# A Mamba and mixture-of-experts kernel: the first guess of each root on one engine, and the block plan's numbers on VectorE

## The chip, the core and the metric

The kernel runs on one core of a Trainium2 chip. A core has a matrix engine (TensorE, PE in the profile; PEld is its weight loads), VectorE (DVE), ScalarE (ACT), GpSimd (POOL) and SyncE (SP), which here only issues transfers. Each engine works through a queue of its own in order; engines wait for each other by semaphores. The metric is the device time of one execution in microseconds. Before the change three runs gave 1625.85, 1628.82 and 1631.47 us, median 1628.82.

## The reference

Input x is 4 sequences of 1024 tokens, 256 wide, all in float32. Two layers follow each other, each with its residual and a layer norm behind it.

```python
h = x * rsqrt(mean(x*x) + 1e-5) * norm_scale
xs, res = split(h @ w_in, 2)                      # 512 channels each
xs = silu(causal_conv(xs, conv_w, 4 taps) + conv_b);  res = silu(res)
delta, B, C = split(xs @ w_xproj, [16, 32])
delta = softplus(delta @ w_dt + b_dt)
s[t] = exp(delta[t] * A) * s[t-1] + delta[t] * xs[t] * B[t]   # 512 channels x 16 states
y = sum over the 16 states of s * C
x = layernorm(2 * x + ((y + xs * D) * res) @ w_out)

n = x * rsqrt(mean(x*x) + 1e-8) * norm_weight
p = sigmoid(n @ router.T);  the best 2 of 8 experts, weights p / (sum of both + 1e-6)
x = layernorm(x + shared_mlp(n) + sum over both of weight * expert_mlp(n))
```

Each MLP is 256 to 1024 to 256 with a relu and biases.

## The kernel before

**Chunks and stages.** A sequence is cut into two chunks of 512 tokens, eight chunks in all. For a chunk, `front` computes the first norm, the projections, the convolution and delta; then 16 scan steps, one for each state n, run over the four blocks of 128 channels (`inputs`, `scan`, `outputs`); then `tail` computes the gate, the output projection, both norms and the routing, and `by_expert` scatters the tokens to the rows of their experts and plans blocks of 128 rows. `moe` works through units of 128 rows, four of the shared MLP and some routed blocks for each chunk. `finish` is the closing layer norm over all tokens, in five pieces.

**A scan step.** PE spreads a row of B or C over the partitions (L427). DVE multiplies three of the four channel blocks by B (L441), POOL the fourth (L446). ACT computes da = exp(delta * A) (L454), DVE runs the recurrence (L457, four a step) and multiplies by C (L470), POOL adds that to y (L471, 128x2048 elements). The product hs has three buffers, da has two in PSUM.

**What runs beside it.** While chunk i is scanned, `front` of chunk i+1, `tail` of chunk i-1 and the units of `moe` are issued in between as generators: after each channel block, the main loop advances them. Which instruction of an engine is issued before which is then settled when the program is built: the framework takes the program order as priority and lets an instruction go when its inputs are there by its own estimate of durations, so that an instruction can go ahead of one written before it, or behind one written after it. Some ACT and DVE instructions are pinned by `keep_in_program_order`.

**The roots.** `rsqrt(v, name, engine)` is called 21 times: in `front` for the mean square `ms` that ACT computed (eight, 128x4 numbers, on POOL but for the first chunk, which uses DVE), in `tail` for both variances of the norms (eight, 128x8, on POOL, from a `var` that POOL computes in L520 to L522), and in `finish` (five, the last on DVE, the others on POOL). It treats the float as an integer: a shift right by one (L204) and a subtraction from a constant (L206) give the first guess, both on DVE, whatever `engine` is. Three Newton steps of four instructions follow on `engine` (L209 to L212).

**The plan.** `by_expert` has the counts of tokens by expert in `place`, a part of one PSUM tile (`pr`). DVE compares them with the multiples of 128 (L681) and sums to the number of full blocks so far (L686); POOL subtracts the blocks done (L687) and multiplies by a triangular matrix of ones, 8x8 for each partition (L689). Then the first choice's four scatters are issued (POOL's indirect DMAs, L646), and after a pause of a turn or two the second choice's. DVE sums the products to each expert's first block (L696) and goes on to the table `plan` (L697 to L721), from which SP's queue reads the expert of a block (L767) and the place of its rows (L793). POOL adds to `done` (L726). Eight plans are made, the last behind the last scan.

The main loop's share that issues `moe`:

```python
            side(ending)
            other_work(LEN[b, c] / MAXC)
```

Of the kernel before, what the change touches and what calls it, by code (L numbers as in the profile page):

```python
# [10 lines left out]
ALU = mybir.AluOpType  # L11
AX = mybir.AxisListType

P = 128
# [6 lines left out]
E = 8  # L21
# [44 lines left out]
I32, U32 = mybir.dt.int32, mybir.dt.uint32  # L66
# [4 lines left out]
def mamba_moe_kernel(  # L71
# [18 lines left out]
    nc = tc.nc  # L90

    const = ctx.enter_context(tc.tile_pool(name="const", bufs=1))
    small = ctx.enter_context(tc.tile_pool(name="small", bufs=2))
# [49 lines left out]
    before = const.tile([P, E, E], F32, tag="before", name="before")  # L143
# [56 lines left out]
    def rsqrt(v, name, engine=nc.gpsimd):  # L200

        shape = list(v.shape)
        half = small.tile(shape, I32, tag="half", name=f"half_{name}")
        nc.vector.tensor_scalar(half, v.bitcast(I32), 1, None, ALU.logical_shift_right)  # L204
        y = small.tile(shape, F32, tag="root", name=f"root_{name}")
        nc.vector.tensor_scalar(y.bitcast(I32), half, -1.0, float(0x5F3759DF), ALU.mult, ALU.add)  # L206
        t = small.tile(shape, F32, tag="nt", name=f"nt_{name}")
        for _ in range(3):
            engine.tensor_tensor(t, y, y, ALU.mult)  # L209
            engine.tensor_tensor(t, t, v, ALU.mult)  # L210
            engine.tensor_scalar(t, t, -0.5, 1.5, ALU.mult, ALU.add)  # L211
            engine.tensor_tensor(y, y, t, ALU.mult)  # L212
        return y
# [47 lines left out]
    def front(b, c):  # L261
# [9 lines left out]
        for t in range(TT):  # L271
            nc.scalar.activation(
                hn[:, t, :], x_sb[:, t, :], AF.Square, accum_out=ms[:, t : t + 1]
            )
        nc.scalar.activation(ms, ms, AF.Identity, bias=eps, scale=1.0 / D)
        rstd = rsqrt(ms, f"r1_{s}", nc.vector if alone else nc.gpsimd)
        for _ in range(3):
            yield
# [203 lines left out]
    def tail(b, c):  # L482
# [38 lines left out]
        nc.gpsimd.tensor_scalar(var[:, 1, :], var[:, 0, :], 1e-8, 0.0, ALU.mult, ALU.add)  # L521
        nc.gpsimd.tensor_tensor(var[:, 1, :], var[:, 1, :], mv[:, :, 1], ALU.add)  # L522
        rstd = rsqrt(var, f"l1_{s}")
        yield from wait(3, 6)
        hn = one.tile([P, TT, W], F32, tag="hn2", name=f"hn2_{s}")
# [87 lines left out]
        nc.scalar.copy(combT, pc)  # L613
        channels[b, c] = (x1T, combT)
        yield from by_expert(b, c, hn, rank, weights, both, sofar, part, flat)

    def by_expert(b, c, hn, rank, weights, both, sofar, part, flat):
# [6 lines left out]
        place = part(TT + 1, E)  # L624
# [18 lines left out]
        def scatter(i):  # L643
            nc.gpsimd.tensor_copy(hn[:, :, WEIGHT : WEIGHT + 1], weights[:, i, :].unsqueeze(2))
            for t in range(TT):
                ins = nc.gpsimd.indirect_dma_start(  # L646
                    rows_of[:, :],
                    bass.IndirectOffsetOnAxis(to[:, i, t : t + 1].bitcast(U32), 0),
                    hn[:, t, :], None,
                ).ins  # L650
                for other in scatters:
                    tc.declare_no_dep(ins, other, reason="no two choices share a row")
                for other in taken_from:
                    tc.declare_no_dep(ins, other, reason="rows behind those of full blocks")
                scatters.append(ins)
# [21 lines left out]
        done = done_of[0]  # L677
        levels = [P, E, CAP // BS]
        over = one.tile(levels, F32, tag="ahead", name=f"over_{s}")
# [3 lines left out]
            level.unsqueeze(1).to_broadcast(levels), ALU.is_gt if last_chunk else ALU.is_ge,  # L683
        )
        there = one.tile([P, E], F32, tag="there", name=f"there_{s}")
        nc.vector.tensor_reduce(there, over, AX.X, ALU.add)  # L686
        nc.gpsimd.tensor_tensor(there, there, done, ALU.subtract)  # L687
        ee = one.tile([P, E, E], F32, tag="ee", name=f"ee_{s}")
        nc.gpsimd.tensor_tensor(ee, before, there.unsqueeze(1).to_broadcast([P, E, E]), ALU.mult)  # L689
        scatter(0)  # L690
        yield from wait(1, 2)
        scatter(1)
# [34 lines left out]
        else:  # L727
            over = one.tile([P, 1], I32, tag="over", name="blocks_over")
# [11 lines left out]
    half = HB // 2  # L740
# [201 lines left out]
    def finish():  # L942
# [34 lines left out]
        for i, (o, dst) in enumerate(pieces):  # L977
            tiles = o.shape[1]
            mv = small.tile([P, tiles, 2], F32, tag="mv2", name=f"mv2_{i}")
            stats(o, mv, slice(0, tiles), f"l2_{i}")  # L980
            var = small.tile([P, tiles], F32, tag="var2", name=f"var2_{i}")
            nc.vector.tensor_scalar(var, mv[:, :, 1], 1e-5, None, ALU.add)
            newton = nc.gpsimd if i + 1 < len(pieces) else nc.vector
            rstd = rsqrt(var, f"l2_{i}", newton)
            shift = small.tile([P, tiles], F32, tag="shift", name=f"shift_l2_{i}")
            newton.tensor_tensor(shift, mv[:, :, 0], rstd, ALU.mult)
            newton.tensor_scalar(shift, shift, -1.0, 0.0, ALU.mult, ALU.add)
            if ahead is not None:
                scale(*ahead)
            ahead = o, dst, rstd, shift  # L990
# [34 lines left out]
    for i, step in enumerate(order):  # L1025
        b, c, n = step
        place = chunks.index((b, c))
# [40 lines left out]
    left = nc.values_load(blocks_over[0][0:1, 0:1], min_val=0, max_val=len(at_end))  # L1068
# [66 lines left out]
```

## Time and profile before

| | |
|---|---|
| median of three runs | 1628.82 us (1625.85 to 1631.47) |
| the profiled execution | 1626.85 us |
| its span, first to last instruction | 1625.2 us |
| mean granted clock of PE | 0.87 |
| busy: PE, DVE, ACT, POOL | 1216.2, 1306.5, 1069.7, 1160.6 us |
| last scan ends | 1396 us |
| DMA | 211.59 MB, 130 GB/s on average |

The costliest groups of the page, as line, engine, operation, tiles, shapes and count, then busy time and the mean in ns of one, then the engine's idle time just before them and what ended most of it:

```profile
L471 POOL TENSOR_TENSOR y<-y,hs 128x2048 f32<-128x2048 f32 x128 | 593.8, 4639 | 79.5 <-DVE hs L470 75.2
L457 DVE TENSOR_TENSOR_SCAN hs<-da,state,hs 128x512 f32<-128x512 f32 x256 | 318.0, 1272 | 17.9 <-ACT da L454 17.3
L470 DVE TENSOR_TENSOR hs<-hs,pb 128x2048 f32<-128x2048 f32 x128 | 291.1, 2275 | 4.2 <-PE pb L427 3.0
```

Busy time counts an instruction from its start to its end, so one that is held after it has started looks long rather than late. Idle time is counted before an instruction and put down to the one whose semaphore came last.

### The profile page before, as it was taken

What the parts mean: (1) busy time and instruction counts of PE and PEld (TensorE: products, weight loads), DVE (VectorE), ACT (ScalarE), POOL (GpSimd) and SP (SyncE); (2) the same over time, 40 slices, a digit from 0 to 9 for tenths busy, and PEclk for the clock granted to TensorE, in tenths of its full rate; (3) what the DMA queues carried; (4) which work ended last, traced back from release to release, by engine and by line L of the source; (5) the groups of instructions that cost most, each with busy time, mean ns of one, the idle gap of its engine ahead of it and who ended that gap; (6) DMA issues with size and microseconds to landing.
All of it is one profiled execution on the core that took longest, in us unless ns stands there. A gap on an engine that the chain in (4) does not pass through costs nothing. (4 is left out here: it accounts for less than half of the span.)

```text
span 1625.2 us, 19982 instructions
## 1 busy us (share of the span) xinstructions
PE 1216.2 (75%) x6216; PEld 918.9 (57%) x6216; DVE 1306.5 (80%) x1451; ACT 1069.7 (66%) x2353; POOL 1160.6 (71%) x896
## 2 busy tenths in 40 slices
PE   5253147875668788978878987788888888899990
PEld 2011023663246666666656755676667677789990
DVE  3899899889997898889998998899999889520005
ACT  5656647785678667777688667876786676354442
POOL 1478986698668876798779976997699787641123
PEclk8585576987789899889999998899899899999995
DMA  4000000151015562366326630574166437559996
GB/s 144 0 0 0 0 13 14 59 172 38 20 35 181 173 185 75 117 202 185 81 66 201 209 105 35 165 240 121 34 192 187 136 90 249 180 167 308 335 278 215
DMA packets 160272, 211.59 MB, mean 130 GB/s; under 512 B 20617, under 2 KB 138130, under 8 KB 160162
## 3 DMA queue, kind: packets, MB, share of 16 engines
q1 hardware_dynamic: 135954, 181.75, 33.6%
q0 software_dynamic: 17216, 21.57, 7.4%
q10 hardware_dynamic: 6992, 6.95, 1.2%
q8 instruction: 51, 0.84, 0.2%
q14 instruction: 59, 0.48, 0.1%
HBM read 178.97 MB, written 31.27 MB: 129 GB/s over the span
## 5 line engine op out<-in xcount | busy, mean ns | idle before, releaser
L471 POOL TENSOR_TENSOR y<-y,hs 128x2048 f32<-128x2048 f32 x128 | 593.8, 4639 | 79.5 <-DVE hs L470 75.2
L454 ACT ACTIVATE da<-delta,chan_sb 128x512 f32<-128x512 f32 x512 | 353.4, 694 | 205.7 <-DVE hs L457 202.2
L868 PE MATMUL pd<-w,h 128*128 128x256 f32 x1600 | 387.8, 387 | 18.0 <-ACT h L848 11.3
L868 PEld LDWEIGHTS pd<-w,h 128*128 128x128 f32 x1600 | 300.0, 194 | 91.6 <-issue 23.6
L457 DVE TENSOR_TENSOR_SCAN hs<-da,state,hs 128x512 f32<-128x512 f32 x256 | 318.0, 1272 | 17.9 <-ACT da L454 17.3
L457 DVE TENSOR_TENSOR_SCAN hs<-da,hs 128x512 f32<-128x512 f32 x256 | 302.7, 1212 | 27.9 <-ACT da L454 27.5
L839 PEld LDWEIGHTS pu<-xT,w 128*128 128x128 f32 x2176 | 270.8, 200 | 64.4 <-ACT xT L822 45.4
L839 PE MATMUL pu<-xT,w 128*128 128x128 f32 x2176 | 276.5, 284 | 26.6 <-ACT xT L822 26.6
L470 DVE TENSOR_TENSOR hs<-hs,pb 128x2048 f32<-128x2048 f32 x128 | 291.1, 2275 | 4.2 <-PE pb L427 3.0
L848 ACT ACTIVATE h<-pu,wb 128x128 f32<-128x128 f32 x800 | 228.8, 368 | 74.1 <-PE pu L839 66.5
L446 POOL TENSOR_TENSOR hs<-xs,b 128x512 f32<-128x512 f32 x144 | 199.8, 1392 | 86.9 <-ACT b L439 64.8
L441 DVE TENSOR_TENSOR hs<-xs,pb 128x1536 f32<-128x1536 f32 (+1 forms) x128 | 213.9, 1671 | 15.3 <-ACT b L439 8.8
L427 PE MATMUL pb<-parts,pick 128*128 128x512 bf16 x256 | 107.0, 421 | 150.7 <-DVE hs L441 60.0
L901 POOL DMA_INDIRECT sums<-rb,xb x68 | 108.2, 1591 | 133.8 <-ACT h L848 41.4
L293 PE MATMUL pi<-hT,w_in_sb 128*128 128x512 f32 x256 | 150.4, 719 | 41.8 <-DVE xs L325 15.1
L839 PEld LDWEIGHTS pu<-x1T,w 128*128 128x128 f32 x1024 | 138.5, 213 | 19.4 <-issue 10.9
L839 PE MATMUL pu<-x1T,w 128*128 128x128 f32 x1024 | 143.5, 299 | 0.0
L219 DVE BATCH_NORM_STATS2 bnst_l<-o 128x6 f32<-128x256 f32 x32 | 12.1, 413 | 145.7 <-DMA o<-sums 145.7
L293 PEld LDWEIGHTS pi<-hT,w_in_sb 128*128 128x128 f32 x256 | 52.5, 221 | 127.5 <-issue 39.9
L439 ACT COPY b<-pb 128x512 f32<-128x512 f32 x128 | 75.5, 590 | 30.1 <-PE pb L427 27.0
L503 PE MATMUL po<-w_out_sb,y 128*128 128x256 f32 x256 | 70.3, 437 | 31.8 <-POOL y L493 27.0
L427 PEld LDWEIGHTS <-pick 128*128 128x128 bf16 x256 | 26.6, 107 | 111.1 <-DVE hs L441 51.7
(187 smaller groups left out, 1401.4 us busy)
## 6 DMA issues: line engine op xcount, KB each, us to landing
w<-in_ew SPq DMA_DIRECT2D x136, 1024.0 KB
w<-in_sw SPq DMA_DIRECT2D x16, 1024.0 KB
xb<-rows SPq DMA_DIRECT2D x68, 129.0 KB
x<-in_x SPq DMA_DIRECT2D x8, 512.0 KB
sums<-summed ACTq DMA_DIRECT2D x8, 512.0 KB
sums<-rs POOLq DMA_DIRECT2D x16, 256.0 KB
o<-sums SPq DMA_DIRECT2D x3, 1024.0 KB
out<-o ACTq DMA_DIRECT2D x3, 640.0 KB
```

Source lines behind the costliest of these rows:

```text
L293: nc.tensor.matmul(pi, lhsT=w_in_sb[:, k, m * P : (m + 1) * P], rhs=hT[:, k, :], start=(k == 0), stop=(k == KD - 1),)
L427: nc.tensor.matmul(pb, lhsT=pick[:, row : row + 1].to_broadcast([P, P]), rhs=scans[b, c][3], start=True, stop=True,)
L441: nc.vector.tensor_tensor(hs[:, 0:on_pool, :], xs[:, 0:on_pool, :], pb.unsqueeze(1).to_broadcast([P, on_pool, TC]), ALU.mult,)
L446: nc.gpsimd.tensor_tensor(hs[:, k, :], xs[:, k, :], copy, ALU.mult)
L454: nc.scalar.activation(da, delta[:, k, :], AF.Exp, scale=chan_sb[:, k, CA + n : CA + n + 1])
L457: nc.vector.tensor_tensor_scan(hs[:, k, :], da, hs[:, k, :], 0.0 if c == 0 else state[:, k, n : n + 1], ALU.mult, ALU.add,)
L470: nc.vector.tensor_tensor(hs, hs, pb.unsqueeze(1).to_broadcast([P, KB, LEN[b, c]]), ALU.mult)
L471: nc.gpsimd.tensor_tensor(y, y, hs, ALU.add)
L839: nc.tensor.matmul(pu[:, i, :], lhsT=w[:, k, at : at + P], rhs=xT[:, k, :], start=(k == 0), stop=(k == KD - 1),)
L848: nc.scalar.activation(t[:, i, :], pu[:, i, :], AF.Relu, bias=wb[:, m : m + 1])
L868: nc.tensor.matmul(pd, lhsT=hidden[h][:, i, :], rhs=w[:, m, :], start=(m == 0), stop=(m == HB - 1 and e is None),)
L901: nc.gpsimd.indirect_dma_start(sums_of[:, :], bass.IndirectOffsetOnAxis(xb[:, TOKEN : TOKEN + 1].bitcast(U32), 0), rb, None, compute_op=AL ...
```

## The change

`rsqrt` makes its first guess in one instruction on `engine`: the integer times -0.5 plus the constant, instead of a shift and a product with -1 plus the constant on DVE. The tile `half` is gone. In `by_expert` the number of full blocks is summed into PSUM (`so_far`, over the first row of `place`, which has been read by then); DVE subtracts the blocks done twice, once into `there` (SBUF, read later by L697 and L725) and once into `left` (PSUM, the second row of `place`), and multiplies `left` by the triangular matrix. POOL no longer takes part ahead of the scatters.

```diff
     def rsqrt(v, name, engine=nc.gpsimd):
 
         shape = list(v.shape)
-        half = small.tile(shape, I32, tag="half", name=f"half_{name}")
-        nc.vector.tensor_scalar(half, v.bitcast(I32), 1, None, ALU.logical_shift_right)
         y = small.tile(shape, F32, tag="root", name=f"root_{name}")
-        nc.vector.tensor_scalar(y.bitcast(I32), half, -1.0, float(0x5F3759DF), ALU.mult, ALU.add)
+        engine.tensor_scalar(
+            y.bitcast(I32), v.bitcast(I32), -0.5, float(0x5F3759DF), ALU.mult, ALU.add
+        )
         t = small.tile(shape, F32, tag="nt", name=f"nt_{name}")
...
         there = one.tile([P, E], F32, tag="there", name=f"there_{s}")
-        nc.vector.tensor_reduce(there, over, AX.X, ALU.add)
-        nc.gpsimd.tensor_tensor(there, there, done, ALU.subtract)
+        so_far, left = place[:, 0, :], place[:, 1, :]
+        nc.vector.tensor_reduce(so_far, over, AX.X, ALU.add)
+        nc.vector.tensor_tensor(there, so_far, done, ALU.subtract)
+        nc.vector.tensor_tensor(left, so_far, done, ALU.subtract)
         ee = one.tile([P, E, E], F32, tag="ee", name=f"ee_{s}")
-        nc.gpsimd.tensor_tensor(ee, before, there.unsqueeze(1).to_broadcast([P, E, E]), ALU.mult)
+        nc.vector.tensor_tensor(ee, before, left.unsqueeze(1).to_broadcast([P, E, E]), ALU.mult)
         scatter(0)
```

## The prediction

> **What bounds the kernel now.** I read the page first, then the windows, then who waits for whom, then the lines that the change touches. The busy line of the page says that VectorE (DVE) is the fullest engine, but it is an average over stages, so the first cut is by stage; the columns are the window, then busy time (and instructions) of PE, PEld, DVE, ACT, POOL, the granted clock, DMA share and GB/s:
>
> ```profile
> PE 1216.2 (75%) x6216; PEld 918.9 (57%) x6216; DVE 1306.5 (80%) x1451; ACT 1069.7 (66%) x2353; POOL 1160.6 (71%) x896
> ...
> 0.00:40.00 40.00, 23.71 (x40) 9.07 (x40) 14.88 (x42) 22.32 (x56) 8.11 (x48) 0.84 0.48 146
> 40.00:1396.00 1356.00, 1008.48 (x4970) 741.12 (x4970) 1252.84 (x1254) 956.73 (x2021) 1086.65 (x733) 0.86 0.36 110
> 1396.00:1420.00 24.00, 19.20 (x100) 16.79 (x100) 8.81 (x18) 4.72 (x18) 10.07 (x12) 0.86 0.42 128
> 1420.00:1585.00 165.00, 162.61 (x1102) 150.29 (x1101) 8.32 (x35) 74.57 (x241) 42.13 (x48) 1.00 0.87 271
> 1585.00:1626.00 41.00, 2.25 (x11) 1.64 (x9) 21.64 (x104) 11.32 (x22) 13.62 (x58) 0.57 0.65 213
> ```
>
> From 40 to 1396 us, until the last scan, DVE is busy 1252.8 of 1356 us; PE, ACT and POOL have 348, 399 and 269 us free there. From 1420 to 1585 us PE works off the expert blocks that are left, 162.6 of 165 us busy. The last 41 us are the closing norm. The order of PE's work follows the scans up to 1396 us, so what DVE saves there moves the later stages forward. The waits say the same; each line is who waited, for whom, the total, the times and the longest (first all engines, then DVE alone from 40 to 1396 us):
>
> ```profile
> ACT da L454 <- DVE hs L457: 202.2, 212, 4.4
> ```
>
> ```profile
> DVE hs L457 <- ACT da L454: 44.8, 20, 5.6
> DVE pr L696 <- POOL ee L689: 12.2, 4, 4.3
> DVE hs L441 <- POOL y L471: 4.8, 2, 2.4
> DVE half_l L204 <- POOL var L522: 1.2, 2, 0.6
> ```
>
> ACT waits for the scans 202 us, the scans for ACT 45 us. The second and fourth line are waits that the change touches. The instructions of the first guess, by source line (shortest, median and longest duration in ns):
>
> ```profile
> L204 DVE TENSOR_SCALAR half_l<-var x13: 154/171/743, 238.8 to 1614.1; 128x8 int32<-128x8 int32 x11, 128x4 int32<-128x4 int32 x2
> L204 DVE TENSOR_SCALAR half_r<-ms x8: 157/492/3555, 6.9 to 941.2; 128x4 int32<-128x4 int32 x8
> ...
> L206 DVE TENSOR_SCALAR root_l<-half_l x13: 140/171/3362, 241.1 to 1614.4; 128x8 int32<-128x8 int32 x11, 128x4 int32<-128x4 int32 x2
> ```
>
> An instruction over four to eight numbers takes 0.16 us, and sometimes 3.5. The timelines of the two engines at the longest one tell why (start, duration):
>
> ```profile
> 601.51 5.12 POOL L471 TENSOR_TENSOR y<-y,hs 128x2048 f32<-128x2048 f32 x1
> ```
>
> ```profile
> 603.11 3.56 DVE L204 TENSOR_SCALAR half_r<-ms 128x4 int32<-128x4 int32 x1
> 606.69 0.17 DVE L206 TENSOR_SCALAR root_r<-half_r 128x4 int32<-128x4 int32 x1
> ```
>
> The shift ends at 606.67, the large POOL addition at 606.63. The one of 3.36 us at 1269.63 ends at 1272.99, POOL's addition (1268.45, 4.51 us long) at 1272.96; the one of 2.23 us at 941.18 ends within 0.02 us of POOL's. DVE is held by POOL, and behind it stand the scans.
>
> **The change, part by part**, against the profiled execution: 1626.85 us, span 1625.2; the median of the runs shown is 2.0 us higher.
>
> *The two guess instructions leave DVE.* In the stage from 40 to 1396 us there are 12 roots (7 tails, 5 fronts), 24 instructions. Counted from each start to that of the next instruction they take 14.8 us: six held ones 2.40 + 3.56 + 0.73 + 2.15 + 0.66 + 3.28 = 12.8 us, the other 18 2.0 us. With the waits for POOL's variance (1.2 us) that is 16.0 us off DVE.
>
> *One guess comes to POOL, ahead of the twelve Newton instructions.* No trace shows an int32 form there; the nearest row is L211 on POOL, the same operation on f32, 0.203 us, with 0.08 us to the next. The bounds are 0.2 us and, if the conversion is slow, three times that; I take 0.28 each, 12 x 0.28 = 3.4 us. POOL has 269 us free in the stage, so I cost it at nothing. POOL no longer waits for DVE's guess (6.7 + 2.5 us in the stage), and instead waits at the guess for ACT's mean square of a front. Queued behind it are the products and additions of the scan (L446, L471), for which DVE waited 4.8 us in all.
>
> *Block numbers and products go from POOL to DVE.* DVE loses the wait at L696, 12.2 us in four places of the stage: the next one late there would be the scan, whose da lies ready (median 2 us before the scan starts). The fifth, 5.5 us at 1447 us, lies beside a PE that is full to 1585 us and waits 2.4 us in all there, so I cost it at nothing; without that cover it is worth at most 5.5. DVE gains three instructions in each of seven plans of the stage. The nearest rows are of the same shapes with one operand in PSUM: L697 (128x8, 0.166 us), L712 (128x8, 0.164), L703 (128x64, 0.206). Start to start these take 0.11, 0.12 and 0.16 us on average, since each overlaps its neighbours; at most the sum of durations, 0.54. I take 0.43, since the three hang on each other: 7 x 0.43 = 3.0 us (bounds 1.4 and 3.8). Could they be held as the guesses were? Of the 245 small instructions of routing and plan on DVE in the stage none took over 0.43 us, which is what 256 elements take (L577), while 6 of the 24 guesses were held; all three new ones read PSUM for one operand, as those rows do. I take no stall.
>
> POOL loses L687 and L689 (0.21 + 0.33 us and two issue gaps of 0.17) in each plan. The second choice's scatters are not moved in the program; the first ones may start earlier, as now POOL waits 13.6 us for L686 in front of them. SP's queue waits for the plan (L793 <- L721) before it loads rows and weights; the plan comes some us earlier, with DMA at 36% of its share in the stage, so nothing is pushed.
>
> (SBUF — State Buffer, section Who interferes with whom, in the Trainium skill: a VectorE scalar operation wholly in SBUF can take a port pair that GpSimd uses too, and whichever comes second waits for the whole of the other's instruction; one with a single SBUF input outside that mode is never held. By that rule the new instructions cost the 3.0 us. Were any small instruction held as often as the guesses were, 21 x 6/24 x 2.1 us = 11 us would come on top and the gain would halve. The 245 rows agree with the page.)
>
> *Ends.* In the startup VectorE's own root loses one instruction, 0.20 us (6.87 to 7.07). In the closing norm the last piece's root, on DVE, loses 0.27 us (1614.15 to 1614.42); the four others trade two DVE instructions and a change of engine against 0.28 us on POOL: nothing. 0.5 us together.
>
> *Sum.* 16.0 + 12.2 - 3.0 = 25.2 us less on DVE before the last scan. Not all arrives: a freed DVE next waits for da (20 waits already) or for PE. The ends are all of it and nothing; the da that lie ready and PE's 348 free us speak for most, and I take four fifths, 20.2, since several of the stalls (2 to 4 us) are longer than the 2 us by which da is ahead. With the 0.5: 20.7 us, 1606.2 us for an execution like the profiled one, 1608 by the median.
>
> **The rivals.**
>
> A. *Half arrives.* The queues are filled anew at build, since every start has shifted; another instruction of DVE is then queued ahead of what it needs, as L696 was, at the price that L696 has now (12.2 us). For it: 90 us of other waits on DVE in the stage, at L457, L441, L630, L511. Against: none of them is tied to the guess or the plan. 1608 + 10 = 1618 us.
>
> B. *It is hidden*: the end is set by PE's total. For it: PE is full from 1420 on, and at 80 to 85% for 200 us before. Against: it waits there for ACT's evictions (L848) and DVE's results. Only the 0.5 us of the ends remain: 1628 us.
>
> C. *POOL becomes the bound* (slower). The chain of 12 Newton instructions takes 3.4 us (245.96 to 249.3) and now starts as soon as the variance is there, ahead of products and additions that it followed before. From 1220 to 1260 us POOL is busy 39.0 of 40 us. If each of the 12 chains held the scan for its 3.7 us with the guess, that is 44 us; it outweighs the gain from six chains on (20.7 / 3.7). At eight: 1608 + 30 = 1638 us. Against: three buffers of hs lie between POOL and the scan, and DVE waited for POOL's addition only twice, 4.8 us.
>
> D. *The change doesn't do what it says*: the guess of ACT-fed fronts waits on POOL as long as it did on DVE. That would leave 16.0 us on DVE saved all the same, and falls under A.
>
> **How the numbers follow.** The forecast 0.52 (from 1600 to 1614: carry between 0.6 and all of it and 3 us more), A with D 0.23, B 0.08, C 0.17. Faster by over 0.3% (5 us, about what a measurement of this kernel can tell from no change) is the forecast and A: 0.75; the same, B: 0.08; slower, C: 0.17. The range runs from 1597 (all 25.7 us, DVE's 4.8 us at POOL's addition gone too, 1 us of the plan at the end) to 1631, which takes in A and B and leaves out most of C and a little below: under 2 in 10.
>
> **What the profile after would show.** Right: no L204 guess on DVE, the longest small DVE instruction of the stage under 0.5 us; no wait of L696 for POOL; the three plan instructions near 0.17, 0.17 and 0.2 us; the POOL guess near 0.2 us; the last scan some 20 us before 1396, and the PE stretch to the end as long as before, 190 us. Wrong: the last scan as early as said and the end not (B); more of "L441 <- POOL y" or "L457 <- POOL hs" (C); more of "L457 <- da" or a new line of the same weight as L696's (A); an int32 guess on POOL of half a us or more.

## The result

| | before | after |
|---|---|---|
| median | 1629.74 us (1625.85 to 1631.47) | 1605.66 us (1604.24 to 1609.34) |
| ratio of the times, 95% interval | | 0.986 [0.984, 0.988] |
| profiled execution | 1626.85 us | 1604.24 us |
| its span | 1625.2 us | 1602.5 us |
| first scan starts, last scan ends | 56.0, 1396.4 us | 51.3, 1372.8 us |
| from the last scan to the end | 228.8 us | 229.8 us |

The changed kernel is 24 us, 1.4%, faster; 1608 was forecast. The profile after, in the same cuts as before. The busy line of its page, then the windows, with the columns window, then busy time (and instructions) of PE, PEld, DVE, ACT and POOL, granted clock, DMA share and GB/s. Lines from L687 on have moved down by up to two.

```profile
PE 1205.6 (75%) x6216; PEld 911.2 (57%) x6216; DVE 1294.8 (81%) x1435; ACT 1069.2 (67%) x2353; POOL 1157.8 (72%) x899
...
0.00:40.00 40.00, 21.30 (x42) 7.89 (x43) 18.77 (x45) 25.25 (x62) 8.46 (x50) 0.90 0.50 146
40.00:1373.00 1333.00, 1001.01 (x4966) 735.42 (x4966) 1238.41 (x1244) 953.20 (x2013) 1083.66 (x731) 0.87 0.38 112
1373.00:1400.00 27.00, 22.56 (x129) 20.14 (x128) 7.96 (x15) 7.55 (x25) 12.51 (x24) 0.94 0.55 167
1400.00:1565.00 165.00, 160.73 (x1083) 147.76 (x1081) 8.79 (x38) 72.36 (x235) 39.59 (x35) 1.00 0.87 264
1565.00:1603.00 38.00, 0.00 (x0) 0.00 (x0) 20.91 (x95) 10.84 (x21) 13.63 (x61) 0.54 0.70 225
```

The stage that ends with the last scan is 23 us shorter, and DVE does 14 us less in it; the 165 us of expert blocks and the closing norm behind it have only moved. Who waited for whom (total, times, longest), first over the whole span, then DVE alone from 40 us to the last scan's end:

```profile
ACT da L454 <- DVE hs L457: 194.6, 221, 3.2
```

```profile
DVE hs L457 <- ACT da L454: 50.4, 24, 5.3
DVE hs L441 <- ACT b L439: 7.9, 7, 3.6
...
DVE hs L441 <- POOL y L471: 4.8, 2, 2.5
```

ACT still waits for the scans, 195 us where it was 202. DVE's waits for POOL's product and variance are gone; its wait for da is 5.6 us more, and its wait for POOL's addition has not moved. The guess by source line (shortest, median and longest ns), and the plan's instructions by shape (count, then busy us and mean ns of one, then idle before):

```profile
L204 POOL TENSOR_SCALAR root_l<-var x12: 192/201/291, 235.4 to 1588.8; 128x8 int32<-128x8 int32 x11, 128x4 int32<-128x4 int32 x1
L204 POOL TENSOR_SCALAR root_r<-ms x7: 192/193/197, 20.0 to 931.1; 128x4 int32<-128x4 int32 x7
```

```profile
L691 DVE TENSOR_TENSOR ee<-before,pr 128x64 f32<-128x64 f32 x8 | 1.6, 201 | 0.0
L689 DVE TENSOR_TENSOR pr<-pr,done 128x8 f32<-128x8 f32 x8 | 1.3, 166 | 0.0
L688 DVE TENSOR_TENSOR there<-pr,done 128x8 f32<-128x8 f32 x8 | 1.3, 163 | 0.2
```

No guess is held any more, and an integer guess costs on POOL what a float instruction of its size costs there. Counted from start to start between the first and the last scan, DVE lost 15.0 us of guesses, 1.2 of waits for the variance and 12.3 of waits for the product, and gained 3.1 us in the plan: 25.4 us less. The scans took 19.0 us less (1340.4 to 1321.4). With 4.6 us in the startup and 1.0 us given back behind the last scan, the span is 22.6 us shorter.

**Where the 25 us arrive, and where a quarter of them goes.** The 128 multiplications by C (L470) stand in the same order in both traces, so the start of each in before, less its start in after, is the lead of the changed kernel. It starts at 4.6 us (the startup), is 3.4 before the first stall, and ends at 23.6:

| stall in before, at | held or waiting, us | lead ahead of it and behind it, us |
|---|---|---|
| 275 guess, 301 product | 2.40 + 3.20 | 3.4, 9.0 |
| 603 guess | 3.56 | 5.7, 9.0 |
| 655 product | 1.74 | 7.3, 13.1 |
| 941 guess | 2.23 | 12.4, 14.4 |
| 994 product | 2.93 | 14.1, 19.0 |
| 1268 and 1270 guess | 0.74 + 3.36 | 19.2, 24.9 |
| 1323 product | 4.31 | 22.7, 26.7 |

Each of these steps stands where a stall was taken away (some are larger than the stall, 5.8 us for 1.74, as the order around them changed too), and for 100 to 200 us at a time between them the lead hardly moves. One rise has no such stall, 3.0 us between 354 and 603 us; in it a wait of DVE for da, at 507 us of before, is 2.97 us where it was 5.64. What is given back goes in a few places: 6.3 us between 307 and 354 us of before (9.0 to 2.7), and 1.7 to 3.1 us behind four of the other steps. The largest is in ACT's timeline (start, duration, idle before and releaser), before and after:

```profile
333.79 0.37 ACT L884 COPY rs<-pd 128x256 f32<-128x256 f32 x1 [0.58 <-DMA sums<-rs]
...
346.62 2.56 ACT L414 ACTIVATE y<-xs,chan_sb 128x512 f32<-128x512 f32 x4 [1.04 <-POOL delta L411]
```

```profile
326.53 0.37 ACT L886 COPY rs<-pd 128x256 f32<-128x256 f32 x1 [3.64 <-DMA sums<-rs]
...
343.94 2.56 ACT L414 ACTIVATE y<-xs,chan_sb 128x512 f32<-128x512 f32 x4 [3.49 <-POOL delta L411]
```

The copy of a shared unit's rows waits for a scatter-add that POOL issued at 320.48 us and that lands 6.0 us later, since both use one buffer; in the new order it stands earlier in ACT's queue and waits 3.64 us instead of 0.58, and L414 waits 3.49 us for POOL instead of 1.04. Behind both stand exponentials: DVE waits 2.34, 0.88 and 5.29 us for da between 325 and 348 us, 8.5 us where it was 4.0. It is the order and no accident of one execution: the two waits are 3.72 and 3.48 us in a second profile of the changed kernel, 3.58 and 3.47 with the plan alone, and 0.83 and 1.20 with the guess alone.

### The profile page after: what moved, and what is told of

It reads as the page before. It is cut to its first block, busy times and chain, and to the rows that moved or that the text cites. A ratio compares the mean times of both kernels' runs of the same rounds, so it can differ in the third digit from the quotient of the medians.

```text
span 1602.5 us, 19985 instructions
## 1 busy us (share of the span) xinstructions
PE 1205.6 (75%) x6216; PEld 911.2 (57%) x6216; DVE 1294.8 (81%) x1435; ACT 1069.2 (67%) x2353; POOL 1157.8 (72%) x899
## 5 line engine op out<-in xcount | busy, mean ns | idle before, releaser
L471 POOL TENSOR_TENSOR y<-y,hs 128x2048 f32<-128x2048 f32 x128 | 596.6, 4661 | 80.3 <-DVE hs L470 80.0
L457 DVE TENSOR_TENSOR_SCAN hs<-da,state,hs 128x512 f32<-128x512 f32 x256 | 317.8, 1270 | 26.1 <-ACT da L454 24.9
L841 PE MATMUL pu<-xT,w 128*128 128x128 f32 x2176 | 278.0, 286 | 26.3 <-ACT xT L824 26.3
L470 DVE TENSOR_TENSOR hs<-hs,pb 128x2048 f32<-128x2048 f32 x128 | 290.8, 2272 | 3.0 <-PE pb L427 1.6
L446 POOL TENSOR_TENSOR hs<-xs,b 128x512 f32<-128x512 f32 x144 | 202.9, 1418 | 80.2 <-ACT b L439 59.6
L841 PEld LDWEIGHTS pu<-x1T,w 128*128 128x128 f32 x1024 | 131.8, 205 | 13.8 <-issue 10.4
L841 PE MATMUL pu<-x1T,w 128*128 128x128 f32 x1024 | 137.3, 291 | 0.0
L439 ACT COPY b<-pb 128x512 f32<-128x512 f32 x128 | 75.4, 589 | 28.1 <-PE pb L427 24.0
L503 PE MATMUL po<-w_out_sb,y 128*128 128x256 f32 x256 | 67.3, 423 | 31.4 <-POOL y L493 26.7
```

The lines of the kernel that those rows point to most:

```text
L446: nc.gpsimd.tensor_tensor(hs[:, k, :], xs[:, k, :], copy, ALU.mult)
L457: nc.vector.tensor_tensor_scan(hs[:, k, :], da, hs[:, k, :], 0.0 if c == 0 else state[:, k, n : n + 1], ALU.mult, ALU.add,)
L470: nc.vector.tensor_tensor(hs, hs, pb.unsqueeze(1).to_broadcast([P, KB, LEN[b, c]]), ALU.mult)
L471: nc.gpsimd.tensor_tensor(y, y, hs, ALU.add)
L841: nc.tensor.matmul(pu[:, i, :], lhsT=w[:, k, at : at + P], rhs=xT[:, k, :], start=(k == 0), stop=(k == KD - 1),)
```

## The experiments

The theory: DVE's queue sets the end; it lost 16 us of guesses (most of it instructions held by POOL) and 12 us of waiting for POOL's product, and three quarters of that arrived. Its rivals: only one of the two parts does it; it is the number of instructions rather than the hold; the roots on POOL cost what DVE gained; the gain comes from the startup. All medians, with the ratio to the kernel before on the same chip:

| kernel | median us | ratio [95%] | first scan | last scan ends | to the end |
|---|---|---|---|---|---|
| after, again | 1607.75 | 0.988 [0.986, 0.991] | 51.7 | 1372.5 | 230.1 |
| after, a third time | 1606.16 | 0.988 [0.985, 0.990] | 52.3 | 1374.5 | 231.0 |
| the guess alone | 1613.58 | 0.992 [0.989, 0.994] | 52.3 | 1378.9 | 230.8 |
| the plan alone | 1617.32 | 0.995 [0.993, 0.997] | 53.8 | 1381.7 | 230.8 |
| one guess instruction, on DVE | 1615.46 | 0.993 [0.991, 0.995] | 50.8 | 1381.3 | 230.4 |
| the last plan on POOL | 1608.69 | 0.987 [0.985, 0.990] | 52.6 | 1373.5 | 234.0 |
| the product from SBUF | 1611.78 | 0.991 [0.988, 0.993] | 51.2 | 1379.6 | 230.8 |
| a fourth Newton step | 1622.67 | 0.997 [0.995, 0.999] | 51.6 | 1383.1 | 237.8 |
| load on POOL | 1608.72 | 0.989 [0.987, 0.991] | 51.2 | 1375.5 | 232.1 |
| two Newton steps | 1603.43 | 0.987 [0.985, 0.989] | 54.4 | 1372.9 | 228.1 |
| the old guess in the startup | 1608.77 | 0.989 [0.986, 0.992] | 56.1 | 1378.2 | 229.6 |

### Each part alone

The first keeps the new guess and the old plan, the second the new plan and the old guess (against the changed kernel):

```diff
-        so_far, left = place[:, 0, :], place[:, 1, :]
-        nc.vector.tensor_reduce(so_far, over, AX.X, ALU.add)
-        nc.vector.tensor_tensor(there, so_far, done, ALU.subtract)
-        nc.vector.tensor_tensor(left, so_far, done, ALU.subtract)
+        nc.vector.tensor_reduce(there, over, AX.X, ALU.add)
+        nc.gpsimd.tensor_tensor(there, there, done, ALU.subtract)
...
-        nc.vector.tensor_tensor(ee, before, left.unsqueeze(1).to_broadcast([P, E, E]), ALU.mult)
+        nc.gpsimd.tensor_tensor(ee, before, there.unsqueeze(1).to_broadcast([P, E, E]), ALU.mult)
```

> The guess in one instruction on its engine, the plan as before. Theory (the held instructions of DVE are the gain): no guess on DVE in the scan, 16.0 us of DVE time gone there, of which three quarters arrive as with the whole change (19.0 of 25.2), so the last scan ends 12 us earlier relative to the first one; the startup (first scan at 56.0 us before, 51.3 after) is shortened by the full 4.7 us; together about 17 us, 1613 us. The wait of DVE for ee on POOL stays near 12 us in total. Rival 1 (the new order of the queues makes the gain): the time does not follow the removed DVE time; all of the 24 us or next to none of it. Rival 2 (POOL's waits for the guess were what counted): 9 us less, 1620.

```diff
+        half = small.tile(shape, I32, tag="half", name=f"half_{name}")
+        nc.vector.tensor_scalar(half, v.bitcast(I32), 1, None, ALU.logical_shift_right)
...
-        engine.tensor_scalar(
-            y.bitcast(I32), v.bitcast(I32), -0.5, float(0x5F3759DF), ALU.mult, ALU.add
-        )
+        nc.vector.tensor_scalar(y.bitcast(I32), half, -1.0, float(0x5F3759DF), ALU.mult, ALU.add)
```

> The plan's numbers and products on DVE, the guess as before, two instructions on DVE. Theory: the wait for ee (12.2 us in the scan) is gone, three instructions in each plan come back (3.1 us measured after), three quarters of 9 us arrive: 7 us, 1622 us; the startup stays at 56.0 us; the guesses are held again, 10 to 15 us over the scan. Rival 1 (order): any other figure, more than 6 us off. Rival 2 (relieving POOL is what counted): POOL loses 0.9 us in each of seven plans and its wait for L686, some 15 us.

Both parts gain, 0.82% and 0.50% by the ratios (13 and 10 us by the medians, where 17 and 7 were expected); together that is 1.32%, beside 1.2 to 1.4% for the whole in its three sets of runs. Each leaves the other's stall in place. With the guess alone, DVE's wait for the product is there:

```profile
DVE pr L696 <- POOL ee L689: 11.6, 4, 3.8
```

With the plan alone, the held guesses are:

```profile
L204 DVE TENSOR_SCALAR half_l<-var x13: 152/163/709, 236.8 to 1601.5; 128x8 int32<-128x8 int32 x11, 128x4 int32<-128x4 int32 x2
L204 DVE TENSOR_SCALAR half_r<-ms x8: 155/496/3515, 6.8 to 936.1; 128x4 int32<-128x4 int32 x8
```

Six instructions of the guess take 0.7 to 3.5 us each there, 13.0 us in all, at the places and for the lengths of the six before (13.1). Between the first and last scan the guess alone takes 13.8 us off where it removed 16.2, the plan alone 12.5 where it removed 9.2 (the wait for ACT's copy, L439, happened to be 6 us less). The two add up to 26.3 us and the whole has 19.0. The timed ratios show no such gap, executions of one kernel lie up to 15 us apart (1618.52 to 1633.83 for the kernel before, on one chip), each length here is read from a single profile, and each build draws its order anew; so whether the parts overlap by some us stays open.

### One instruction, or its engine

The guess stays one instruction and is on DVE for every root:

```diff
-        engine.tensor_scalar(
+        nc.vector.tensor_scalar(
             y.bitcast(I32), v.bitcast(I32), -0.5, float(0x5F3759DF), ALU.mult, ALU.add
```

> After, but the one-instruction guess always on DVE. Theory (an instruction of DVE wholly in SBUF is held by the large additions of POOL): of the 12 guesses in the scan about a quarter are held, 2 us each, so 6 us plus 1 us for the rest are back on DVE: three quarters of it arrive, 1611 us against 1606. Rival (the number of instructions counts, not the engine): the guesses take 0.17 us each, time as after, 1606. The gap of PE in the startup (2.7 us after, 3.1 us before) should lie near 2.9 us; whether the clock falls there is open.

The guess by source line in this kernel, then the instruction on DVE that is held longest and what POOL does then (start, duration):

```profile
L204 DVE TENSOR_SCALAR root_l<-var x13: 152/165/712, 235.4 to 1600.6; 128x8 int32<-128x8 int32 x11, 128x4 int32<-128x4 int32 x2
L204 DVE TENSOR_SCALAR root_r<-ms x8: 158/496/3503, 6.8 to 935.6; 128x4 int32<-128x4 int32 x8
```

```profile
600.61 3.50 DVE L204 TENSOR_SCALAR root_r<-ms 128x4 int32<-128x4 int32 x1
```

```profile
599.00 5.07 POOL L471 TENSOR_TENSOR y<-y,hs 128x2048 f32<-128x2048 f32 x1
```

The guess ends at 604.11, POOL's addition at 604.07. Five of the twelve guesses of the stage are held, 9.7 us in all (2.41, 3.50, 0.82, 2.23, 0.71); the scans take 9 us longer than in the changed kernel, and the ratio is 0.5 to 0.7% worse. Halving the number of instructions leaves most of the stall: it is the engine that pays. I had expected three held ones, and 1611 us; a single guess meets POOL's long instructions as often as a pair does: the six held ones of before lie in five pairs.

### Where the product's operands lie

The new plan keeps one operand of its instructions in PSUM. Here the second copy is gone, and the product takes both operands from SBUF:

```diff
-        so_far, left = place[:, 0, :], place[:, 1, :]
+        so_far = place[:, 0, :]
...
-        nc.vector.tensor_tensor(left, so_far, done, ALU.subtract)
...
-        nc.vector.tensor_tensor(ee, before, left.unsqueeze(1).to_broadcast([P, E, E]), ALU.mult)
+        nc.vector.tensor_tensor(ee, before, there.unsqueeze(1).to_broadcast([P, E, E]), ALU.mult)
```

> After without the copy in PSUM: the product with the triangular matrix takes both operands from SBUF. Theory (an instruction of DVE with two operands in SBUF waits for a POOL instruction that reads SBUF): two or three of the seven products in the scan are held, 1 to 4 us each, 5 us in all, 0.8 us are saved by the instruction left out; 1609 us. Rival (only the small scalar operations wholly in SBUF are held): the product stays at 0.2 us, time as after or 1 us less.

The product by its source line (L690 here; shortest, median and longest ns), then the longest one and POOL's work beside it:

```profile
L690 DVE TENSOR_TENSOR ee<-before,there x8: 200/345/1553, 293.1 to 1424.3; 128x64 f32<-128x64 f32 x8
```

```profile
647.58 1.55 DVE L690 TENSOR_TENSOR ee<-before,there 128x64 f32<-128x64 f32 x1
```

```profile
647.77 1.27 POOL L446 TENSOR_TENSOR hs<-xs,b 128x512 f32<-128x512 f32 x1
```

Of eight products three take 1.14 to 1.55 us, each up to the end of such an L446 (649.13 against 649.04 here), and a fourth takes 0.45, up to the end of an L471; with an operand in PSUM the longest of eight takes 0.22. One instruction fewer (0.7 us over the stage) thus costs 3.8 us at the product, and the scans take 6 to 8 us longer; how much of the rest is the new order stays open. The page "SBUF — State Buffer" of the Trainium skill, section "Who interferes with whom", says that a VectorE instruction with two SBUF inputs contends with a GpSimd instruction that reads SBUF, and one with at most one SBUF input, outside the two-port modes, does not; this case's traces agree with both halves (1.55 and 0.22 us).

### The last plan

The prediction cost the eighth plan's wait at nothing, since PE is full beside it. Here it alone goes back to POOL:

```diff
+        if last_chunk:
+            nc.vector.tensor_reduce(there, over, AX.X, ALU.add)
+            nc.gpsimd.tensor_tensor(there, there, done, ALU.subtract)
+            nc.gpsimd.tensor_tensor(ee, before, there.unsqueeze(1).to_broadcast([P, E, E]), ALU.mult)
+        else:
```

> After, but the last chunk's plan (behind the last scan) with its two operations on POOL as before. Theory (PE has work enough there): the plan is 5 us later and the time the same within 3 us, 1606. Rival (the plan's start sets the end): 5 us more, 1611.

The plan is done 53.7 us after the last scan instead of 48.5, and PE ends 190.5 us after it in both: PE is the cover, as said. In the profile the end came 3 to 4 us later all the same, behind a later last scatter-add (issued 196.3 us after the last scan, 191.7 to 193.6 us in the kernels without added work on POOL); but before and the guess alone have that plan on POOL too, and 191.9 and 192.9. The time, 0.987 [0.985, 0.990], is that of the changed kernel. What made that one scatter-add late I have not found.

### What the roots cost on POOL

Three kernels, each against the changed one. A fourth Newton step in every root on POOL, 48 instructions and 10.1 us of busy time more in the twelve chains before the last scan (13.5 us with the gaps between them, by the estimate ahead of the run); the same 48 instructions behind the chains, on a tile that nobody reads, 10.2 us; and one Newton step fewer:

```diff
-        for _ in range(3):
+        for _ in range(4 if engine is nc.gpsimd else 3):
```

> After with four Newton steps in place of three for every root on POOL: 4 instructions of 0.28 us more for each, 13.5 us more of POOL in the scan, 4.5 us in the closing norm. Theory (POOL has room in the scan): the scan is 1321 us long as after, within 4 us; the closing norm, where the pieces wait for POOL, is 1 to 4 us longer; 1609 us. Rival (POOL is now the bound): the scan is longer by most of 13.5 us, 1622.

```diff
+    def load_pool(y, name):
+
+        pad = small.tile(list(y.shape), F32, tag="pad", name=f"pad_{name}")
+        for _ in range(4):
+            nc.gpsimd.tensor_tensor(pad, y, y, ALU.mult)
...
+        if not alone:
+            load_pool(rstd, f"r1_{s}")
...
+        load_pool(rstd, f"l1_{s}")
```

> After with four further POOL multiplications on a spare tile behind each root of fronts and tails: the same 13.5 us of POOL in the scan as the fourth Newton step, but nobody waits for them. Theory (the fourth step lengthened the scan by 10 us because ACT's pinned scaling L243 stood waiting for the end of POOL's chain, 10.5 us against 1.7, and da behind it): the scan within 4 us of 1321, L243's wait within 3 us of 1.7; 1609 us. Rival (POOL's load itself carries over): the scan 1331 us long, as with four steps; 1618.

```diff
-        for _ in range(3):
+        for _ in range(2):
```

> After with two Newton steps in place of three for every root (the relative error of the root is then some 5e-6). Theory (only the end of the chain counts, and ACT waits 1.7 us for it now): at most 2 us less in the scan, 1 to 3 us less in the closing norm; 1603 us. Rival (POOL's load counts): the scan 10 us shorter, 1594.

The wait of ACT for the second norm's shift, which POOL computes at the end of a Newton chain: before, after, the fourth step, and the load behind the chain.

```profile
ACT hn L243 <- POOL shift_n L240: 7.0, 3, 3.7
```

```profile
ACT hn L243 <- POOL shift_n L240: 1.7, 3, 1.1
```

```profile
ACT hn L243 <- POOL shift_n L240: 10.5, 3, 7.7
```

```profile
ACT hn L249 <- POOL shift_n L246: 2.3, 3, 1.3
```

The fourth step costs 15 us (1622.67 beside 1607.75 on the same chip, where I had expected 1609); in the profile 10.8 us lie in the scans and 7.7 behind them, where the roots of the closing norm have the fourth step too. The load behind the chains has no part in the closing norm, so the scans are what can be compared: they are 2.1 us longer with it than in the run beside it (1324.3 and 1322.2), and its time is 3 us longer (1608.72 beside 1606.16, within the intervals). So POOL's free time does take up most of such work, but not a delay at the end of a chain: L243 is one of the ACT instructions pinned in program order, and what stands behind it on ACT waits too. Its longest wait in the kernel with the fourth step (start, duration, idle before and releaser):

```profile
1265.78 1.58 ACT L243 ACTIVATE hn<-summed,shift_n,root_l 128x256 f32<-128x256 f32 x3 [7.68 <-POOL shift_n L240]
```

Behind it the scans run 6.5 us later than in the changed kernel beside it; 4.5 of that are made good by 1310 us, and at the last scan 10.8 are missing. DVE waits 10.5 us more in all between the first and the last scan, 7.5 of them for da; how much of this goes back to L243 stays open. One step fewer has no such wait left in the stage and 3 us shorter scans, and its time cannot be told from that of the changed kernel: three steps, with the guess on POOL, already end early enough. The new guess shortens this chain itself, since POOL no longer waits for DVE at the head of it: ACT's wait is 7.0 us with the old guess and the new plan, 6.5 with the one-instruction guess on DVE, and 1.7 in the changed kernel.

### The startup

The first scan starts 4.6 us earlier, for which the prediction had 0.2. The first three roots get their old guess back:

```diff
+        if name in ("r1_0_0", "r1_0_1", "r1_1_0"):
+            half = small.tile(shape, I32, tag="half", name=f"half_{name}")
+            nc.vector.tensor_scalar(half, v.bitcast(I32), 1, None, ALU.logical_shift_right)
+            nc.vector.tensor_scalar(
+                y.bitcast(I32), half, -1.0, float(0x5F3759DF), ALU.mult, ALU.add
+            )
+        else:
```

> After, but the first three roots (the fronts of chunks 0, 1, 2, all before the first scan) with two instructions on DVE as before. Theory (the startup gained because PE's gap ahead of the second half of the w_xproj products fell from 3.1 to 2.7 us, and its clock no longer halved there): gap 3.1 us, the four products 2.5 to 3.8 us instead of 2.0, first scan at 54 to 56 us, the scan 1321 us long as after; 1609 us. Rival (the earlier first scan is chance from run to run): first scan near 51 us.

> The changed kernel once more, beside the next three on one chip: ratio to before 0.986, no guess on DVE in the scan, first scan near 51 us, scan 1321 us long.

> The changed kernel a third time, beside these two: ratio to before 0.986 to 0.988, first scan between 51 and 52 us, PE's gap in the startup 2.7 us.

The second half of the w_xproj products on PE: before, after, and with the old guess in the startup (start, duration, idle before).

```profile
28.72 3.78 PE L360 MATMUL pp<-xs,w_xp_sb 128*128 128x512 f32 x4 [3.07 <-ACT xs L329]
```

```profile
27.32 1.98 PE L360 MATMUL pp<-xs,w_xp_sb 128*128 128x512 f32 x4 [2.73 <-ACT xs L329]
```

```profile
28.88 3.78 PE L367 MATMUL pp<-xs,w_xp_sb 128*128 128x512 f32 x4 [3.07 <-ACT xs L336]
```

The same four products take 3.78 us behind a gap of 3.07 us and 1.98 behind one of 2.73. The granted clock (third figure from the end) gives the reason; the windows are the end of the gap in before, and the whole gap in after:

```profile
27.37:28.72 1.35, 0.00 (x0) 0.00 (x0) 1.35 (x3) 0.66 (x2) 0.00 (x0) 0.50 0.00 0
```

```profile
24.59:27.32 2.73, 0.00 (x1) 0.00 (x0) 2.67 (x5) 1.41 (x6) 1.77 (x9) 1.00 0.00 0
```

In before PE runs these products at half its clock (0.50), in after at the full one (1.00). They start 1.4 us earlier in after; the other 3.2 of the 4.6 us come behind their start. With the old guess in the startup the first scan starts at 56.1 us again, 4.4 us later than in the run of the changed kernel beside it, and its profiled execution takes 1609.54 against 1604.28. The medians are only 1.0 us apart (1608.77 and 1607.75), with intervals of some 4 us on either side. So the slower products are in the traces, and come back with the old guess; how much of the 24 us they make in most executions stays open.

## Why the prediction was right, point by point

- *The two guess instructions leave DVE, 16.0 us*: 16.2 by the same count. The cause it named, POOL holding DVE, is shown by the guess on DVE, which is held as one instruction too.
- *One guess comes to POOL, costed at nothing*: the size was right, 0.19 to 0.20 us, and so was the free time (the load behind the chain). The step named the wrong ones behind it: L446 and L471 lost nothing (DVE's wait for L471 is 4.8 us in both), and the one that waits for the end of the chain is ACT's pinned L243. It gained, by 5.3 us of waits, as the chain no longer waits for DVE's guess.
- *Block numbers and products*: 12.3 us of waits gone for 12.2, 3.1 us added for 3.0. That the new instructions are not held was right, and for the product the operand in PSUM is the reason: with two in SBUF four of eight were held, three of them for about 1 us.
- *The fifth wait, costed at nothing*: right; PE ends at the same distance from the last scan with that plan on either engine.
- *Four fifths arrive*: 19.0 of 25.4, three quarters, stall by stall. The next late thing was da, as said (5.6 us more); why it was late was not foreseen: at the largest place, two ACT instructions that wait 5.5 us longer, for a transfer and for POOL, in the new order.
- *Ends, 0.5 us*: this term was mis-sized. The startup's 0.20 became 4.6 in the profile, 3.2 of it behind the start of the products that PE then ran at full clock, which the prediction did not look at in the first 40 us; the 0.27 us of the closing norm are not to be seen, and the stretch behind the last scan is 1.0 us longer. The two errors, the carry (1.2 us too much) and the ends (3.1 too little), are of opposite sign: 20.7 us became 22.6. That the total came within 2 us is in part luck.

Of the rivals, *half arrives* has something in it: an instruction did come to stand ahead of what it needs, but on ACT instead of DVE, and at 6.3 us instead of 12.2. *Hidden by PE* is out: the stretch from the last scan to the end is 229 to 231 us in before, after and with either part alone, wherever the last scan lies. *POOL becomes the bound* is out at this size, and the fourth Newton step shows how near it was: one more step costs 10.8 us in the scans and 7.7 behind them, while DVE's wait for L471 grew by 1.1 us only.

## What to carry to other kernels

A small VectorE instruction whose busy time reaches from 0.16 to 3.5 us is to be read beside GpSimd's timeline: if its end falls on the end of a GpSimd instruction, move it to GpSimd, as the guess here, or, where it has two operands, put one in PSUM, as for the product; making one instruction of two helped little (9.7 us held instead of 13.1). What a chain of small instructions costs on an engine with free time is set by who waits for its last one, above all if that one stands in a queue with a fixed order. And when stalls are taken away, lay the starts of the same instruction in both traces beside each other: the steps show which stalls paid, and the drops where something new waits.

## What was not expected of the hardware

In all thirteen profiles TensorE's clock went with the idle gap ahead of those four products: nine profiles with a gap of 2.73 us ran them at the full clock, in 1.98 us, and four with a gap of 3.07 us had half the clock for some or all of them, 2.48 to 3.78 us. But the length of this gap alone does not tell when the clock falls. In three of the four the granted clock is down 1.7 to 2.1 us into the gap, sooner than the nine gaps ended that left it up; in the fourth, the plan alone, it falls 1.4 us behind the gap's end. The four also have more idle time just ahead, 0.3 to 0.5 us in gaps around the first half of the products, where the nine have 0.1. What decides it stays open. The page "TensorE: Matmul & The Clock Gate" of the Trainium skill, Part 1, puts the clock's fall at one idle window of about 3.4 us; here it fell around a gap of 3.07 us, mostly before that gap was over.
